# Linear attention: where the two transpositions of the next batch stand in TensorE's order, which engine copies them out, and three small products in one PSUM bank

## The chip, the cores and the metric

The kernel runs on one core of one Trainium2 chip. The metric is the device time of one execution in microseconds; the median of three runs of the kernel before is 1341.5 us (1340.82 to 1342.1).

## What is computed

A transformer-like block on `x` of shape (4, 512, 256), fp32 throughout: a mixture of experts, then linear attention added to `x`, then a softmax attention with a gate and a field term, then two layers of local attention with feed-forward, added to `x`. The change lies in the linear attention and in the first part ("front") of the attention that follows. Of the reference:

```python
qkv = x @ w_qkv.T                     # linear attention; x here: the experts' output
q, k, v = to_blocks(split(qkv))       # 8 heads of 32, blocks of 32 tokens
qp = elu(einsum('bhcsd,hdf->bhcsf', q, proj)) + 1.0
kp = elu(einsum('bhcsd,hdf->bhcsf', k, proj)) + 1.0
kv = einsum('bhcsf,bhcsd->bhcfd', kp, v)
num = einsum('bhcsf,bhcfd->bhcsd', qp, kv)
z = 1.0 / (einsum('bhcsf,bhcf->bhcs', qp, kp.sum(axis=3)) + 1e-08)
out = (num * z[..., None]) @ w_out.T + b_out
...
coh = sigmoid(tanh(comb @ Wc1.T + bc1) @ Wc2.T + bc2)   # next attention: the gate
mod = (1.0 - fi) * mod + fi * fa[:, None, :, None]      # the field term
```

## The kernel before

Stages follow one another: experts, linear attention, conditioned attention, local attention. The framework's list scheduler orders each engine's instructions at compile time from program order and its own estimate of when data are ready, and gives a tile the bank that it takes for free. TensorE is an exception: inside `PE.in_order()` every matmul and transposition keeps the program's order (L72 to L93). `pinned(...)` (L1215) holds one instruction behind the one that the program has just before it on its engine; it is a lower bound on its place, not an exact one.

The linear attention works on the 4 batches one after another. PSUM has 8 banks: 4 make up two double banks `fe` for features, 4 form the pool `mm` for all else (L1771, L1772).

`front(b)` (L1778) is a generator that prepares a batch in pieces, one for each `yield`: it combines the experts' results (`weighted`, `g` and `ymoe`), starts the loads for a later batch (`results`), then two turns (four transpositions each into a bank `pt`, copied to `yT`), four products `pqk` copied to `qk` (in the order 0, 2, 1, 3), and two products `pv` copied to `v`. `evac` (L124) gives these copies to ScalarE and VectorE in turn, so the first half of `yT` is copied by ScalarE and the second by VectorE.

The main loop (L1901) has a step `k` for each batch `b` and pair of heads `u` from 0 to 3. Its functions:

- `features(d, u)`: 4 products `pf` (32 rows each) into the two double banks; on ScalarE relu and exp for each (`ex`), on VectorE `f` from `pf` and `ex`. `f` frees the double bank.
- `scores(d, u)`: 8 products of 128 by 128 into two banks `psc`, masked on VectorE into `sc`.
- `values(d, g)`: the products `pn` and `pz` with `sc`, into one bank each; ScalarE copies `pz` to `z`, VectorE takes the reciprocal (3.35 us) and multiplies to `aT`. `pn` is held until then.
- `tail`: output product `pao` of a batch, added to `x`.

Between these the loop takes pieces from `fill`: the next batch's front and the last batch's tail (`beside`, L1879), or, in the last batch, the front of the conditioned attention for its batch 0 (`cond_front`, L285). An even step has three places (behind the values, behind the features, behind the scores), an odd one the last two: ten places for ten pieces. So a step with `u = 0` has, in TensorE's order: last values of the batch before, turn, features, turn, scores, first `pqk`. For the first batch these pieces stand elsewhere: its own `pv` take the first places and the next batch's turns come in step 1.

`cond_front` has two turns as well (copied to `xT2` by ScalarE for batch 0; VectorE sums the copies into `xs`), then products for keys, queries, gate and values. At its end stand small products: `pch` (the gate, L355), copied to `chT`; `pvs` (the sums of the values, L364), from which `vs` and `vsB` are made; `pchT` (the turn of `chT`, L373), from which `coh` is made; and `pvw` (L388) with `vsB`. Each takes a bank of its own through `acct`, which in this stage is the pool `mm`. Behind them TensorE has the last batch's last values, and then the next stage, whose scores `sc` have 5 banks and whose other products have 3.

## Time and profile before

| what | value |
| --- | --- |
| median of the runs | 1341.5 us (1340.82 to 1342.1) |
| the profiled execution: its own time | 1343.32 us |
| its span, first to last instruction | 1341.6 us |
| mean granted TensorE clock | 0.983 |
| linear attention in the span | about 305 to 465 us |
| reciprocal on 128x512 (L1856) | 3.35 us |
| copy of a turn: ScalarE, VectorE | 0.58, 0.68 us |
| relu and exp on 128x1024 (L1819, L1820) | 1.02, 1.06 us |
| `f` on 128x1024 (L1822) | 1.22 us |

A timeline row has the start in the span, the duration, the engine (PE is TensorE's matmul, PEld its weight load, DVE VectorE, ACT ScalarE, POOL GpSimd), the line, the operation, output and inputs by tile names, and the shape; in brackets stands the idle time before it and what ended it. Rows of like instructions are merged, with a count. A row of windows gives, for each stretch, its length, each engine's busy time and the granted clock. Products and transpositions go through helpers, so their lines are L82 and L86 and they are told apart by tiles.

### The profile page before, as it was taken

Reading aid. Unit: us, or ns where it says so; the run is one execution under the profiler, and the core shown is the slowest. Engines: PE = TensorE matmul, PEld = TensorE weight load, DVE = VectorE, ACT = ScalarE, POOL = GpSimd, SP = SyncE. Lnnn points to the kernel's source line nnn. Section 1 sums busy time; section 2 is a strip of 40 time slices with the busy share of each in tenths; the row PEclk is TensorE's granted clock in tenths of the full one; section 3 lists DMA queues with packets and bytes.
Section 4 is the critical chain, followed back from the end, with each engine's and each line's share of the span. In section 5 each row is a group of like instructions: output and inputs, shape, how many; then the busy total and the mean of one; then the engine's idle time right before and its main releaser. Section 6 shows DMA issues by size and latency. Waiting matters only on the chain.

```text
span 1341.6 us, 23073 instructions
## 1 busy us (share of the span) xinstructions
PE 1271.8 (95%) x9214; PEld 812.2 (61%) x9214; DVE 683.4 (51%) x1464; ACT 581.4 (43%) x1157; POOL 292.9 (22%) x321
## 2 busy tenths in 40 slices
PE   4899999998999999999999999999999998999998
PEld 3788899964566634344344655766555556667654
DVE  6221243425777733242237788654372877864421
ACT  3221233326655365646644646561222655463111
POOL 1322356420000101010103334210030333422010
PEclk7899999998999999999999999999999999999999
DMA  3565666523000000000210001311001011012000
GB/s 96 213 236 192 236 239 221 189 76 116 1 1 1 1 1 1 0 1 1 91 57 14 18 18 27 104 34 25 24 0 43 25 30 30 18 43 56 18 21 22
DMA packets 41856, 85.29 MB, mean 64 GB/s; under 512 B 9409, under 2 KB 25673, under 8 KB 39433
## 3 DMA queue, kind: packets, MB, share of 16 engines
q1 hardware_dynamic: 36600, 73.02, 16.9%
q0 software_dynamic: 3504, 9.46, 2.1%
q8 instruction: 77, 1.26, 0.4%
q10 hardware_dynamic: 1632, 1.21, 0.3%
q14 instruction: 43, 0.34, 0.1%
HBM read 74.76 MB, written 6.82 MB: 61 GB/s over the span
## 4 chain that ended last, share of the span: by engine, by line
PE 75%; DVE 9%; DMA 6%; ACT 5%; issue 3%; POOL 1%; SPq 0%; DVEq 0%; POOLq 0%
PE ph L82 11%; PE pdq L82 7%; PE pfy L82 6%; PE sc L82 6%; PE pua L82 5%; PE pug L82 5%; PE pv L82 5%; PE pdy L82 4%; PE po L82 3%; PE pn L82 3%; DMA ys<-ob,goal 2%; PE pds L82 2%; PE pqk L82 1%; PE pz L82 1%; PE pqt L86 1%
## 5 line engine op out<-in xcount | busy, mean ns | idle before, releaser
L82 PE MATMUL pdq<-wqkv,yT 128*128 128x512 f32 x384 | 171.7, 597 | 2.4 <-DVE t L626 2.2
L424 ACT ACTIVATE cex<-sc 128x512 f32<-128x512 f32 x256 | 132.2, 604 | 85.6 <-PE sc L82 84.6
L82 PEld LDWEIGHTS pdq<-wqkv,yT 128*128 128x128 f32 x384 | 71.1, 190 | 84.6 <-issue 76.1
L82 PE MATMUL ph<-h,w 128*128 128x256 f32 (+2 forms) x576 | 121.5, 370 | 0.3 <-ACT h L1596 0.3
L629 POOL TENSOR_TENSOR qr<-t,t 128x512 f32<-128x512 f32 x64 | 81.3, 1271 | 140.5 <-DVE t L626 140.5
L82 PEld LDWEIGHTS ph<-h,w 128*128 128x128 f32 x576 | 102.0, 192 | 15.2 <-ACT h L1596 0.5
L1461 DVE TENSOR_SCALAR h<-ph,w 128x256 f32<-128x256 f32 (+2 forms) x52 | 23.0, 461 | 121.8 <-PE ph L82 101.7
L394 POOL TENSOR_SCALAR fterm<-vw,faT 128x256 f32<-128x256 f32 x16 | 14.6, 920 | 317.6 <-DVE cr L384 317.6
L82 PE MATMUL sc<-qm,kT 32*128 32x512 f32 x512 | 82.6, 639 | 0.0
L681 ACT ACTIVATE p<-pds,ss 128x192 f32<-128x192 f32 (+1 forms) x256 | 79.8, 425 | 2.1 <-PE pds L82 0.8
L82 PE MATMUL pua<-hT,w 128*128 128x512 f32 x160 | 75.3, 593 | 0.9 <-DVE z L706 0.9
L82 PE MATMUL pug<-hT,w 128*128 128x512 f32 x160 | 76.2, 598 | 0.0
L619 ACT ACTIVATE sq<-pdq 128x512 f32<-128x512 f32 x64 | 38.5, 601 | 83.7 <-POOL qr L629 42.2
L714 POOL TENSOR_TENSOR p<-p 128x192 f32<-128x192 f32 x64 | 42.4, 682 | 138.1 <-PE pn L82 135.3
L796 ACT ACTIVATE gl<-pug,cols 128x512 f32<-128x512 f32 x40 | 27.3, 687 | 93.6 <-PE pug L82 90.8
L82 PE MATMUL pv<-cex,v 128*32 128x512 f32 x512 | 61.9, 598 | 2.7 <-DVE vw L391 2.7
L82 PE MATMUL pfy<-w,uA 128*128 128x256 f32 x256 | 61.4, 383 | 0.0
L82 PE MATMUL po<-w,h 128*128 128x256 f32 x264 | 60.1, 380 | 0.0
L82 PE MATMUL pdy<-wo,oT 128*128 128x256 f32 x256 | 58.9, 383 | 0.0
L684 DVE TENSOR_TENSOR p<-p,lmask 128x384 f32<-128x384 f32 x64 | 47.0, 735 | 23.0 <-ACT p L681 21.6
L82 PE MATMUL pn<-p,v 64*64 64x128 f32 (+1 forms) x1792 | 50.3, 254 | 8.2 <-DVE p L687 4.2
L1459 ACT ACTIVATE h<-ph,w 128x256 f32<-128x256 f32 (+2 forms) x52 | 22.4, 455 | 81.9 <-PE ph L82 78.0
(352 smaller groups left out, 2329.8 us busy)
## 6 DMA issues: line engine op xcount, KB each, us to landing
w<-in_moe_w_dram SPq DMA_DIRECT2D x18, 1024.0 KB, 7.9
w<-in_moe_w_dram SPq DMA_DIRECT2D x18, 516.0 KB, 4.0
w<-in_moe_w_dram SPq DMA_DIRECT2D x14, 640.0 KB, 4.5
zb<-rows SPq DMA_DIRECT2D x32, 256.0 KB, 4.1
g<-ys SPq DMA_DIRECT2D x6, 512.0 KB, 6.9
wqkv<-in_f_wqkv_dram SPq DMA_DIRECT2D x2, 1536.0 KB
w<-in_f_w_dram SPq DMA_DIRECT2D x2, 1408.0 KB
w<-in_moe_w_dram SPq DMA_DIRECT2D x4, 512.0 KB
```

Source lines behind the costliest of these rows:

```text
L82: cls._queue(nc.tensor.matmul(*args, **kw))
L86: cls._queue(nc.tensor.transpose(*args, **kw))
L394: nc.gpsimd.tensor_scalar_mul(fterm[:, t, :], vw, W["faT"][:, t, b : b + 1])
L424: nc.scalar.activation(ex[:, i, :], pss[2 * j + i], AF.Exp, scale=CHD**-0.5)
L619: nc.scalar.activation(sq, p3, AF.Square)
L629: nc.gpsimd.tensor_tensor(qr_t[:, s], t1, t2, ALU.add)
L681: nc.scalar.activation(p[:, j * 192 : j * 192 + n], pss[j // 2][r][:, j % 2 * 192 : j % 2 * 192 + n], AF.Exp, scale=d.ss[:, j, 1, 2 * c + ...
L684: nc.vector.tensor_tensor(edges, edges, lmask[:, :128].rearrange("p (s q) -> p s q", q=64).unsqueeze(1).to_broadcast([128, 3, 2, 64]), ALU ...
L714: nc.gpsimd.tensor_tensor(p[:, 1:, 0:64], p[:, 1:, 0:64], p[:, : NT - 1, 128:], ALU.add)
L796: nc.scalar.activation(gl, pg, AF.Gelu, bias=col("bg", l * (NU + 1) + i))
L1459: pinned(nc.scalar.activation(dst, src, AF.Relu, bias=bias))
L1461: pinned(nc.vector.tensor_scalar(dst, src, bias, 0.0, ALU.add, ALU.max))
```

## The change

Three edits. In `cond_front`, for batch 0, the sums and the turn of `chT` go to free columns of the bank that holds `pch`; other batches keep their banks. In `front`, the batches behind the first copy both turns by ScalarE, pinned. In the loop, the first step of each batch but the first takes two pieces directly behind the values and none behind the features, so that both turns stand ahead of the features.

```diff
-        ps = acct("pvs")
+        sums = ps[:, 128:130] if b == 0 else acct("pvs")[:, 0:2]
         for c in range(2):
-            mm(ps[:, c : c + 1],
+            mm(sums[:, c : c + 1],
                [(W["wqkv"][:, k, 2 * H + c * 128 : 2 * H + (c + 1) * 128], xs[:, k : k + 1]) for k in range(2)])
         vs = tile_of(temp, [128, 2], "vs")
-        nc.vector.scalar_tensor_tensor(vs, bv2, float(S), ps[:, 0:2], ALU.mult, ALU.add)
+        nc.vector.scalar_tensor_tensor(vs, bv2, float(S), sums, ALU.mult, ALU.add)
         vsB = tile_of(temp, [128, 2, 128], "vsB")
         nc.vector.tensor_copy(vsB, vs.unsqueeze(2).to_broadcast([128, 2, 128]))
         yield
-        ps = acct("pchT")
-        PE.transpose(ps[:, 0:128], chT, ident)
+        turned = ps[:, 256:384] if b == 0 else acct("pchT")[:, 0:128]
+        PE.transpose(turned, chT, ident)
         C3 = [128, NT, CH]
         coh = tile_of(keep, C3, "coh")
         nc.vector.tensor_tensor(
-            coh, ps[:, 0:128].rearrange("p (t h) -> p t h", h=32)[:, :, 0:CH],
+            coh, turned.rearrange("p (t h) -> p t h", h=32)[:, :, 0:CH],
             row("bc2").unsqueeze(1).to_broadcast(C3), ALU.add)
...
                         PE.transpose(pt[:, k * 128 : (k + 1) * 128], y[b][:, k, c * 128 : (c + 1) * 128], ident)
-                    evac(yT[:, c, :], pt)
+                    if b:
+                        pinned(nc.scalar.copy(yT[:, c, :], pt))
+                    else:
+                        evac(yT[:, c, :], pt)
                     yield
...
                         values(ds[b0], u0 // 2)
                         next(fill, None)
+                        if u == 0:
+                            next(fill, None)
                     if k + 1 < len(steps):
                         b1, u1 = steps[k + 1]
                         features(ds[b1], u1)
-                    next(fill, None)
+                    if u or k == 0:
+                        next(fill, None)
                     if b < B:
                         scores(ds[b], u)
                     next(fill, None)
```

## The prediction

> **What bounds the kernel now.** I read the page first, from the busy shares down:

> ```profile
> PE 1271.8 (95%) x9214; PEld 812.2 (61%) x9214; DVE 683.4 (51%) x1464; ACT 581.4 (43%) x1157; POOL 292.9 (22%) x321
> ```

> TensorE is the bound; VectorE and ScalarE matter only where TensorE waits for them. The linear-attention stage runs from about 305 to 465 us. So I next asked for the busy time in three of its stretches, each from one first turn to the next (the last ends at the last values):

> ```profile
> core 0: us, PE busy (x) PEld busy (x) DVE busy (x) ACT busy (x) POOL busy (x), PEclk, DMA share, GB/s
> 354.50:390.10 35.60, 33.41 (x285) 22.16 (x281) 25.83 (x26) 19.69 (x22) 0.00 (x0) 1.00 0.01 1
> 390.10:425.60 35.50, 33.34 (x281) 22.11 (x280) 25.83 (x26) 19.70 (x22) 0.00 (x0) 1.00 0.00 1
> 425.60:463.00 37.40, 35.63 (x247) 23.49 (x246) 27.82 (x34) 17.27 (x21) 0.00 (x0) 1.00 0.00 1
> ```

> The granted clock is full (1.00) and DMA is silent, so neither is in play. TensorE is idle 2.2, 2.2 and 1.8 us: 6.1 us in all. No reordering here can win more than about that, 0.45% of the kernel. Where it lies is in the timeline, TensorE first, from the first turn of the batch at 354.5 us:

> ```profile
> 354.50 0.66 PE L86 MATMUL pt<-ident,ymoe 128*128 128x128 f32 x4
> 355.08 1.14 PE L82 MATMUL pf<-qk,aproj 32*128 32x512 f32 x8
> 356.15 0.66 PE L86 MATMUL pt<-ident,ymoe 128*128 128x128 f32 x4
> 356.65 1.95 PE L82 MATMUL psc<-f 128*128 128x128 f32 x16
> 359.55 1.13 PE L82 MATMUL pqk<-yT,awqkv 128*128 128x512 f32 x2 [0.96 <-DVE aT L1857]
> 361.28 1.12 PE L82 MATMUL pqk<-yT,awqkv 128*128 128x512 f32 x2 [0.60 <-DVE yT L129]
> 362.34 1.29 PE L82 MATMUL pf<-qk,aproj 32*128 32x512 f32 x8
> ```

> The first product pqk waits twice: for a bank (pn's, free when aT is done) and for the second turn's copy. VectorE shows why both are late:

> ```profile
> 355.35 3.35 DVE L1856 RECIPROCAL z<-z 128x512 f32<-128x512 f32 x1 [1.94 <-ACT z L1851]
> 358.81 0.69 DVE L1857 TENSOR_TENSOR aT<-pn,z 128x512 f32<-128x512 f32 x1
> 359.42 1.22 DVE L1822 SCALAR_TENSOR_TENSOR f<-pf,ex 128x1024 f32<-128x1024 f32 x1
> 360.55 0.68 DVE L129 COPY yT<-pt 128x512 f32<-128x512 f32 x1
> 361.14 1.22 DVE L1822 SCALAR_TENSOR_TENSOR f<-pf,ex 128x1024 f32<-128x1024 f32 x1
> ```

> The copy, whose data are there at 356.8, stands behind the 3.35 us reciprocal. The boundary at 390.1 has the same waits (0.93 and 0.60).

> **The turns and their copies, boundaries at 354.5 and 390.1.** Nothing is added to TensorE: pt, pf, pt becomes pt, pt, pf, and psc still starts at 356.65. ScalarE gains a copy of 0.58 (its own first copy's row) in each of three batches, VectorE loses one of 0.68. No DMA is moved: the result loads are still issued with the first turn. The pin holds the first copy behind the batch's four g on ScalarE; all 16 of those are done by 321.6.

> ScalarE: second copy about 355.75 to 356.3; pf now ends 0.5 later, at 356.7, so the four passes of relu and exp start at 356.73 instead of 356.26 and end at 360.84 instead of 360.37. What is queued behind them are the two f on VectorE. The first f starts at 359.42 as before, because aT holds it. The second could start at 360.88; but between the two f the VectorE queue has a hole, where the compile-time list scheduler put the copy, and I expect it to put a masking (sc, 0.64) there. Then the second f stands at 361.16 to 362.38, as late as before.

> TensorE: psc takes 1.78 to the next start, so pqk starts at 358.43 (a turn's bank is free by 356.3) and is through at 360.34. That wins 2.0. But the next pf needs the two feature banks that the two f empty: its first half goes at 360.69, its second at 362.43. A split pf is seen in the row of the third boundary below: its second half starts at 433.85 and the next piece 1.06 later. So the next pqk starts at 363.49 instead of 363.56: the wait for a bank and a copy turns into a wait for f, and the win shrinks to 0.07 here.

> It comes back one step on. The first half's features are ready at 361.83, so relu starts at 361.87 instead of 363.51; four passes later (365.98 instead of 367.63) the last f ends at about 367.3 and the maskings at 368.5 instead of 370.08. The values before waited for these: 368.98 to 372.00, 3.02 us, against 1.88 without a wait (352.61 to 354.49). Now they start at 368.91, wait for nothing and end at 370.79: **1.2 us won at each of the two boundaries, -2.4 together**. Bounds for each: 0.6 if both maskings go ahead of the second f (362.98), 1.5 if none does. If pqk still gets pn's bank and waits to 359.5, the same counting gives 0.9. The following odd step has its own stall of about 1.2 (values at 388), set by the chain from its own pf; it moves along and gives nothing.

> **The third boundary, 425.6.** Here the fill is the first front of the next attention; its copies are ScalarE's already.

> ```profile
> 431.00 1.98 PE L82 MATMUL pck<-xT,cwqkv 128*128 128x512 f32 x4 [1.27 <-DVE aT L1857]
> 432.91 2.07 PE L82 MATMUL pf<-qk,aproj 32*128 32x512 f32 x8
> ```

> pck can start at 429.56 and loses its wait, but VectorE works from 426.46 to 435.0 without a hole: reciprocal, xs 0.63, aT, f, xs 0.68, f (432.59 to 433.80), maskings. All of it but the maskings stands ahead of the second f in the new order too, so pf's second half still starts at 433.85. Value 0; bounds -0.6 (an xs behind the f) and +0.6 (a masking ahead of it).

> **The first batch's copy (330 to 336).** The slots don't move; the second copy leaves VectorE (334.94 to 335.62) for ScalarE, idle from 333.8 to 335.96. The product that reads it starts at 335.79 after the values. Value 0, bounds 0.3 either way.

> **Three products in one bank.**

> ```profile
> 460.24 1.05 PE L82 MATMUL pvs<-xs,cwqkv 128*128 128x1 f32 x8
> 460.38 0.28 DVE L361 COPY chT<-pch 128x128 f32<-128x128 f32 x1
> 461.16 0.31 PE L86 MATMUL pchT<-ident,chT 128*128 128x128 f32 x1
> 461.33 0.16 DVE L369 SCALAR_TENSOR_TENSOR vs<-cols,pvs 128x2 f32<-128x2 f32 x1 [0.66 <-PE pvs L82]
> ```

> Before, pvs is written while chT is read, in two banks. By these rows the sharing costs nothing. [...] Behind pvw on TensorE stand the last values. [...] I take **+0.5**. A gain could come only from a bank that is free earlier: pvw's wait of 0.50 ends with coh, and vsB is done at 461.81, so at most 0.1.

> **The handover to the next stage.** With two fewer banks taken, the last pn and pz may lie in other banks. The next stage's second score waits 0.58 for z now, its second turn 0.59 for aT. Value 0; bounds -1.2 (both waits gone) and +3.9 (the slower rival below).

> **Sum:** -2.4 + 0 + 0 + 0.5 + 0 = -1.9 us. The profiled execution has a span of 1341.6 and a time of its own of 1343.3; the median is 1341.5. A difference of 1.9 is the same against either, so from the median: **1339.6 us**.

> **Rivals.** A difference of 0.2% (2.7 us) is about what a measurement of this kernel can tell from no change.
> - *More is freed* (chance 0.25): no masking ahead of the second f (1.5 twice), and one handover wait gone (0.6) or an xs behind its f. -3.0 + 0.5 - 0.6 = -3.1: 1338.4; with everything, -4.3: 1337.2. For it: VectorE is idle enough. Against: the queue fills that hole in the rows shown.
> - *The change doesn't do what it says* (0.17): f takes the whole of the place of the removed waits, because both maskings go ahead. -1.2 + 0.5: 1340.8. For it: in the first batch (332.60) two maskings do stand ahead of the second f. Against: there a copy stood between relu and exp and made the hole wider.
> - *Slower* (0.13): the next stage's second score, released at 465.71 by z, gets pn's bank instead. That one is free only when aT is done at 469.71, behind 3.4 us of reciprocals. TensorE keeps its order, so it stands 4.0 longer: -1.9 + 4.0 = +2.1, 1343.6. It decides from a wait over 1.9. For it: the second turn waits for that bank now, so the scheduler hands it out too early. Against: only one of the four banks goes to the scores.
> - The forecast itself has 0.45, with its own bounds 1338.4 to 1340.8.

> Range 1337.0 to 1342.4: from everything freed to the nearer part of the slower case. Faster by over 0.2% (below 1338.8): most of the first rival and a fourth of my own case, 0.33. Slower (above 1344.2): only the slower rival with a further cost, 0.09. Within: 0.58.

> **What the changed profile would show.** Right: pqk without a wait at the first two boundaries, the next pf split in two by a wait for f of about 1.7 us, and the values one step on taking 1.9 us instead of 3.0; pvs starting after chT's end. Wrong: pqk still waiting for aT or yT; a stretch from first turn to first turn shorter by much more than 1.2 us, or not at all; a gain in the third stretch; a new wait of sc or pt for aT after 463 us. All would be wrong if the schedule of later stages changed.

## The result, and the profile after

The changed kernel takes 1343.3 us (median of 21 runs, 1341.38 to 1346.93); the kernel before, run in turn with it, takes 1341.2 us (21 runs, 1335.94 to 1342.16). The ratio is 1.0023, with a 95% interval of 1.0016 to 1.003: slower by about 0.2%, and the interval leaves out no change. The forecast was 1339.6, a little faster.

The profiled execution of the changed kernel has a span of 1342.7 us and a time of its own of 1344.44. The three stretches that the prediction shows look, in the windows view, much as before, but for one figure (columns: start and end, length, busy time of TensorE, its weight load, VectorE, ScalarE and GpSimd with counts, granted clock, DMA share, GB/s):

```profile
354.50:390.10 35.60, 33.69 (x311) 22.64 (x304) 25.21 (x25) 20.18 (x23) 0.00 (x0) 1.00 0.00 1
390.10:425.60 35.50, 33.62 (x246) 21.45 (x243) 25.07 (x25) 20.18 (x23) 0.00 (x0) 0.95 0.00 1
425.60:463.00 37.40, 35.75 (x294) 23.95 (x282) 26.74 (x30) 17.02 (x20) 0.00 (x0) 1.00 0.01 2
```

In the second row the clock is 0.95, where before all three rows had 1.00. More of TensorE's time is busy than before in both of the first two rows (33.69 against 33.41, 33.62 against 33.34); in the second, part of that is work at half speed. I come back to this.

First the order of the work. TensorE's timeline at the first boundary of the changed kernel (this profile runs 0.80 us later here than that of before; lines from `front` on have moved by 3):

```profile
355.30 1.09 PE L86 MATMUL pt<-ident,ymoe 128*128 128x128 f32 x8
356.33 1.14 PE L82 MATMUL pf<-qk,aproj 32*128 32x512 f32 x8
357.40 2.05 PE L82 MATMUL psc<-f 128*128 128x128 f32 x16
359.29 1.88 PE L82 MATMUL pqk<-yT,awqkv 128*128 128x512 f32 x4
361.49 1.13 PE L82 MATMUL pf<-qk,aproj 32*128 32x512 f32 x4 [0.32 <-DVE f L1825]
363.91 1.13 PE L82 MATMUL pf<-qk,aproj 32*128 32x512 f32 x4 [1.29 <-DVE f L1825]
```

Both turns stand together, `pqk` waits for nothing, and the next `pf` is split in two by a wait for `f` (1.29 us, where about 1.7 was expected): signs that the prediction named. So is the next one, the values one step on, from `pn` to the product behind them in 1.89 us instead of 3.02:

```profile
370.38 0.42 PE L82 MATMUL pn<-sc,v 128*32 128x128 f32 x8
372.27 1.98 PE L82 MATMUL pqk<-yT,awqkv 128*128 128x512 f32 x4
```

VectorE shows how late the second `f` is:

```profile
359.62 0.69 DVE L1860 TENSOR_TENSOR aT<-pn,z 128x512 f32<-128x512 f32 x1
360.22 1.21 DVE L1825 SCALAR_TENSOR_TENSOR f<-pf,ex 128x1024 f32<-128x1024 f32 x1
361.36 1.28 DVE L1835 TENSOR_TENSOR sc<-psc,bmask 128x512 f32<-128x512 f32 x2
362.55 1.21 DVE L1825 SCALAR_TENSOR_TENSOR f<-pf,ex 128x1024 f32<-128x1024 f32 x1
```

Between the two `f` stand both maskings (x2, 1.28), not one. The second `f` begins at 362.55, with the 0.80 taken off 0.6 us later than I had it.

The small products at the end of the stage, TensorE, changed kernel:

```profile
460.91 0.64 PE L82 MATMUL pch<-cT,cwc 128*32 128x128 f32 x16
461.96 1.05 PE L82 MATMUL pch<-xs,cwqkv 128*128 128x1 f32 x8 [0.41 <-DVE chT L361]
463.27 0.33 PE L86 MATMUL pch<-ident,chT 128*128 128x128 f32 x1 [0.25 <-DVE vs L369]
463.60 1.13 PE L82 MATMUL pvw<-cwout,vsB 128*128 128x256 f32 x4
```

All three go to one tile, and each waits until VectorE has read the one before: the sums begin 0.06 us after `chT`'s end (461.90). Before, `pvw` waited 0.50 for `coh` in the same place, so the net price is 0.40. Behind them the next stage's second score and second turn, which waited 0.58 and 0.59 before, wait for nothing now. Of the kernel before, `pvw` and the second turn:

```profile
461.96 1.10 PE L82 MATMUL pvw<-cwout,vsB 128*128 128x256 f32 x4 [0.50 <-DVE coh L377]
469.76 0.66 PE L86 MATMUL pt<-ident,xres 128*128 128x128 f32 x4 [0.59 <-DVE aT L1857]
```

and of the changed kernel, the second turn:

```profile
472.00 0.66 PE L86 MATMUL pt<-ident,xres 128*128 128x128 f32 x4
```

To sum this up I compared the start of the same instruction in both timelines at each end of a part, and took off 1.7 us for each stretch of half speed within it (below). By the order of its work the changed kernel wins 1.1 at the first two boundaries and 0.2 at the third, loses 0.4 at the small products and wins 0.8 at the handover: -1.7 us. Yet it is slower. Ahead of these parts and behind them, half speed taken off in the same way, the profiles don't tell the two kernels apart: up to the first turn at 354.5 the kernel before takes 339.1 us and the changed kernel 338.2 and 340.2 in two profiles (the second is e5's), and from the handover to the end 863.1 against 863.4 and 861.5. Executions of one kernel differ by 2 us there, so a smaller change of order elsewhere is not excluded. What the records do show is the clock.

### The profile page after: what moved, and what is told of

Read it like the earlier page. It is cut to its first block, busy times and chain, and to the rows that moved or that the text cites. A ratio compares the mean times of both kernels' runs of the same rounds, so it can differ in the third digit from the quotient of the medians.

```text
span 1342.7 us, 23072 instructions
## 1 busy us (share of the span) xinstructions
PE 1275.4 (95%) x9214; PEld 814.3 (61%) x9214; DVE 682.0 (51%) x1461; ACT 582.7 (43%) x1160; POOL 292.9 (22%) x321
## 3 DMA queue, kind: packets, MB, share of 16 engines
q0 software_dynamic: 3504, 9.46, 2.1%
## 4 chain that ended last, share of the span: by engine, by line
PE 77%; DVE 9%; DMA 6%; ACT 4%; issue 2%; POOL 0%; SPq 0%; DVEq 0%; POOLq 0%
PE ph L82 11%; PE pdq L82 7%; PE pfy L82 6%; PE sc L82 6%; PE pua L82 5%; PE pug L82 5%; PE pv L82 5%; PE pdy L82 4%; PE po L82 3%; PE pn L82 3%; DMA ys<-ob,goal 2%; PE pqk L82 2%; PE pds L82 2%; PE pqt L86 1%; PE pz L82 1%
## 5 line engine op out<-in xcount | busy, mean ns | idle before, releaser
L82 PE MATMUL pdq<-wqkv,yT 128*128 128x512 f32 x384 | 171.7, 596 | 2.4 <-DVE t L626 2.2
L82 PEld LDWEIGHTS pdq<-wqkv,yT 128*128 128x128 f32 x384 | 71.0, 190 | 84.6 <-issue 76.1
L82 PE MATMUL ph<-h,w 128*128 128x256 f32 (+2 forms) x576 | 121.3, 369 | 0.3 <-ACT h L1596 0.3
L82 PEld LDWEIGHTS ph<-h,w 128*128 128x128 f32 x576 | 101.7, 192 | 15.4 <-ACT h L1596 0.5
L82 PE MATMUL sc<-qm,kT 32*128 32x512 f32 x512 | 82.7, 641 | 0.0
L82 PE MATMUL pua<-hT,w 128*128 128x512 f32 x160 | 75.3, 593 | 1.2 <-DVE z L706 1.2
L82 PE MATMUL pug<-hT,w 128*128 128x512 f32 x160 | 76.1, 598 | 0.0
L82 PE MATMUL pv<-cex,v 128*32 128x512 f32 x512 | 61.9, 598 | 2.7 <-DVE vw L391 2.7
L82 PE MATMUL pfy<-w,uA 128*128 128x256 f32 x256 | 61.4, 383 | 0.0
L82 PE MATMUL po<-w,h 128*128 128x256 f32 x264 | 60.1, 380 | 0.0
L82 PE MATMUL pdy<-wo,oT 128*128 128x256 f32 x256 | 59.3, 384 | 0.0
L82 PE MATMUL pn<-p,v 64*64 64x128 f32 (+1 forms) x1792 | 50.3, 254 | 7.2 <-DVE p L684 3.5
```

Of the source, the lines that this page charges most:

```text
L82: cls._queue(nc.tensor.matmul(*args, **kw))
```

## Where the time went: the clock

TensorE's granted clock falls to half in two places of the changed kernel's stage: from 400.2 and from 465.0 us. In the profile of before it does so nowhere between 335 and 480 us. The windows view, asked for stretches of 3.41 us, of the changed kernel:

```profile
396.77:400.18 3.41, 2.12 (x9) 0.56 (x8) 2.36 (x4) 2.53 (x4) 0.00 (x0) 1.00 0.00 0
400.18:403.59 3.41, 3.41 (x5) 1.33 (x5) 0.87 (x1) 1.99 (x2) 0.00 (x0) 0.50 0.00 0
461.62:465.03 3.41, 2.82 (x29) 2.16 (x33) 1.78 (x8) 0.26 (x1) 0.00 (x0) 1.00 0.00 0
465.03:468.44 3.41, 3.41 (x64) 3.02 (x56) 1.08 (x4) 0.40 (x1) 3.10 (x4) 0.50 0.00 0
```

and of the kernel before, at its emptiest place of the first boundary:

```profile
358.00:361.41 3.41, 1.85 (x9) 0.83 (x8) 3.31 (x5) 2.34 (x3) 0.00 (x0) 1.00 0.00 0
361.41:364.82 3.41, 3.41 (x13) 1.32 (x14) 2.14 (x3) 1.86 (x3) 0.00 (x0) 1.00 0.00 0
```

In the second row of the first fence five rows of products fill 3.41 us. The `pqk` there takes 3.62 us, against 1.98 one boundary earlier:

```profile
364.97 1.98 PE L82 MATMUL pqk<-yT,awqkv 128*128 128x512 f32 x4
399.98 3.62 PE L82 MATMUL pqk<-yT,awqkv 128*128 128x512 f32 x4
```

The busy share doesn't tell what releases it. The window at 358.0 of before was busy for 1.85 us and nothing followed; the one at 396.8 of after was busy for 2.12, its longest gap 1.29, and half speed followed. What differs is what the products do. A row of `psc` streams 128 columns, and 16 rows take 1.78 us to the next start: 0.87 ns per column; four rows of `pqk` with 512 columns take 1.82: 0.89. With 0.88, four rows of `pqk` count 4 x 512 x 0.88 ns = 1.80 us; but the four rows of half a `pf` have 32 rows where `pqk` has 128 (`32*128` and `128*128` in the timeline), so I count them as 1.80 / 4 = 0.45 us, in 1.13 of busy time. Added up over a window and divided by 3.41 this gives an activity, which is my estimate from the shapes and these times (products with 32 columns where `pqk` has 128 are weighted likewise, and a row across an edge is shared by its time on each side). The window at 396.8 is two halves of `pf` with waits around them: 0.26. The one at 358.0 has `psc` and `pqk` in it: 0.44. These are the windows of the grid between 335 and 1331 us in 13 traces (before, after and eleven experiments), without those that are themselves at half speed:

| activity of a window | followed by half speed |
| --- | --- |
| under 0.30 | 31 of 31 |
| 0.30 to 0.35 | 8 of 10 |
| 0.35 to 0.40 | 6 of 17 |
| 0.40 to 0.45 | 1 of 22 |
| 0.45 to 0.60 | 0 of 164 |
| over 0.60 | 0 of 3504 |

The counts in the middle rows move by a few with the way in which a row across an edge is shared. Laid on every place of the grid, the table gives an estimate of how many half-speed stretches an execution of the changed kernel has between 335 and 480 us: 2.0 and 1.8 from its two profiles (1.2 to 1.4 at the first two boundaries, 0.4 at the third, 0.3 at the small products), which is 3.1 to 3.5 us, against 0.04 for the kernel before. The table comes from the same traces, so this checks the size alone.

The waits on the split `pf` are short, at most 1.29 us; still the changed kernel loses up to 1.7 us, by the estimate above, each time that a window of an activity under 0.30 falls there (0.26 at 396.8).

Since the grid lies elsewhere in each execution, one profile can't give the cost. The mean over runs can: each run has its granted clock, and I take span times (1 - clock) as the clock time that it lost. Within one kernel, a lost us goes with 0.68 us of time (254 runs of 11 kernels, correlation 0.69), so taking all of it is an upper measure. In the runs of e5 (below), which have the clock for both, the kernel before lost 18.7 us (35 runs) and the changed kernel 22.1 (12 runs): 3.4 more. With -1.7 from the order that makes +1.7, or +0.6 with 0.68 of it; measured were +2.4 in the mean (+0.7 to +4.4).

## The experiments

The columns of this table: the order's sum (as above, from one profile, clock taken off), the difference in lost clock time (mean over runs), their sum, and the measured difference of the means from the kernel before, all in us; then the ratio with its interval, which is not the ratio of the means. Each has 6 to 22 runs, against 29 to 36 of before on the same chip (e1 to e4 on one, e5 to e8 on a second, e9 to e11 on a third).

| kernel | order | clock | sum | measured | ratio |
| --- | --- | --- | --- | --- | --- |
| e5: the changed kernel again | -1.7 | +3.4 | +1.7 | +2.4 | 1.0019 (1.0005 to 1.0033) |
| e1: turns alone | -0.5 | +4.5 | +4.1 | +5.1 | 1.0039 (1.0025 to 1.0052) |
| e2: shared bank alone | -0.4 | +1.3 | +0.9 | +1.2 | 1.0003 (0.9994 to 1.0012) |
| e3: e1, maskings last | +0.6 | +3.3 | +3.9 | +3.7 | 1.0031 (1.0021 to 1.0041) |
| e4: idle products, banks moved | +2.0 | +4.7 | +6.7 | +8.5 | 1.0065 (1.0052 to 1.0078) |
| e6: idle products, banks kept | -1.7 | +1.0 | -0.7 | +1.1 | 1.0005 (0.9991 to 1.0019) |
| e7: maskings last, two boundaries | -3.6 | +1.6 | -2.0 | -2.1 | 0.9983 (0.9969 to 0.9997) |
| e8: changed, maskings last | -2.8 | +3.2 | +0.4 | +0.1 | 0.9997 (0.9985 to 1.001) |
| e9: copies alone | -0.7 | +0.5 | -0.2 | +0.7 | 1.0011 (0.9995 to 1.0027) |
| e10: places alone | -1.7 | +1.9 | +0.2 | 0.0 | 1.0001 (0.9984 to 1.0018) |
| e11: e7 again | -3.6 | +1.2 | -2.4 | -2.2 | 0.9991 (0.9977 to 1.0005) |

Order and clock together come within 1.0 us of the measured difference in nine of the eleven rows; e4 and e6, the two with idle products, miss it by 1.8.

All but e2 are given as edits of the changed kernel, unless another is named.

**e1: the turns alone.** The three small products keep their banks.

```diff
-        sums = ps[:, 128:130] if b == 0 else acct("pvs")[:, 0:2]
+        sums = acct("pvs")[:, 0:2]
...
-        turned = ps[:, 256:384] if b == 0 else acct("pchT")[:, 0:128]
+        turned = acct("pchT")[:, 0:128]
```

> The early turns with ScalarE's copies, each small product in its own bank as before. My theory: the changed kernel loses by TensorE's clock. Both maskings stand ahead of the second f, so pf is split by a wait of 1.3 us between two halves that use only half of the array's rows, and in some executions the next clock window of 3.4 us is granted half speed, which costs 1.7 us; 0.5 us is won at each of the first two boundaries. Then this kernel stands between -1 and +1.5 us of the kernel before, with a half-speed window between 360 and 405 us in some profiles, and below the changed kernel by 0.5 to 2. Rival: the sharing of the bank, and what it does to the banks of the next stage, is the whole loss. Then this kernel is 1.1 us faster than before.

A miss: it is the slowest but one, 5.1 us over before, and slower than the changed kernel, not faster. The boundaries give what they gave (-1.1, and -0.4 at the third), but at the handover the next stage's first turn now waits for `aT`, since it was given the bank of `pn`:

```profile
467.87 1.12 PE L86 MATMUL pt<-ident,xres 128*128 128x128 f32 x4 [2.87 <-DVE aT L1860]
```

and the profile has four windows at half speed between 335 and 480 us, two of them from 466.4 us on, as it ends. (The halves of `pf` work on 32 rows where `pqk` works on 128: a quarter, not half.)

**e2: the shared bank alone**, as an edit of the kernel before: only the lines of `cond_front`.

```diff
-        ps = acct("pvs")
+        sums = ps[:, 128:130] if b == 0 else acct("pvs")[:, 0:2]
...
-        ps = acct("pchT")
+        turned = ps[:, 256:384] if b == 0 else acct("pchT")[:, 0:128]
```

> Only the shared bank; turns and copies as before. My theory: the wait for chT and for vs costs 0.4 us on TensorE, and the window of the small products (at about 460 us) becomes a half-speed candidate, so +0.4 to +2 us against the kernel before. Rival (the sharing is the whole loss): +3 us in every execution, with a wait behind the handover to the next stage. Third possibility (sharing frees banks and the handover waits go): within 0.3 us.

The order loses 0.4 at the small products and wins 0.8 at the handover, as in the changed kernel: both belong to this edit. Its profile has one half-speed stretch there, from 464.9 us, behind the small products, as in the changed kernel, and it loses 1.3 us more to the clock. By the ratio's interval the time can't be told from before.

**e3: the maskings behind the second `f`**, on e1, in the first step of the batches behind the first.

```diff
-                    nc.vector.tensor_tensor(sc, psc.rearrange("p (t q) -> p t q", q=128), cw_["bmask"], ALU.mult)
+                    masked = nc.vector.tensor_tensor(sc, psc.rearrange("p (t q) -> p t q", q=128), cw_["bmask"], ALU.mult)
+                    if u == 0 and d is not ds[0]:
+                        pinned(masked)
```

> The early turns without the shared bank, and the two maskings of the first step of each later batch pinned behind the second f. My theory: the second f ends 1.2 us earlier, the split of pf shrinks to less than 0.5 us of wait in its second half, each of the first two boundaries wins 1.3 to 1.5 us, no half-speed window there: 2 to 3 us faster than the kernel before. If the order of f and the maskings were not the failing step, it stands like the early turns alone, within 0.5 us.

A miss: a faster kernel was expected, and it is 3.7 us over before. The boundaries did gain: -3.0 for the first two instead of -1.1. But the next stage's second score was given `pn`'s bank. TensorE's timeline of e3 at the handover:

```profile
457.58 1.12 PE L82 MATMUL sc<-qm,kT 32*128 32x512 f32 x2
462.56 1.41 PE L82 MATMUL sc<-qm,kT 32*128 32x512 f32 x6 [3.85 <-DVE aT L1862]
```

This is the slower rival of the prediction (4.0 there, 3.85 here), in another kernel than the one that it was written for.

**e4: idle products in the hole**, a first trial of the clock: three times five products of `ident` with itself, each five in a bank of their own, between the two halves of the split `pf` at the first two boundaries and ahead of `pf` at the third.

```diff
+            def warm(n):
+                t = mmt("pwarm")
+                for _ in range(n):
+                    PE.matmul(t[:, 0:128], ident, ident, start=True, stop=True)
...
+                    if u == 2 and d is not ds[0] and s == (d is not ds[3]):
+                        warm(5)
```

> The changed kernel with 15 more matmuls of 128 by 128 on the identity matrix, whose result nobody reads: 5 in the wait between the halves of pf in each of the first two boundaries and 5 ahead of pf in the third, about 1.1 us each, so that TensorE works while it would wait. If half-speed windows are what it loses: 1 to 3 us faster than the changed kernel, although it does more work, and no half-speed window at 360 to 440 us. If the clock has no part: as slow as the changed kernel or up to 0.5 us slower.

Also a miss in the time, which says little of the clock: the three extra tiles turned the banks, the second score waits 3.9 us for `aT` as in e3, and the kernel is 8.5 us over before, of which 1.8 stay unaccounted for. As expected, though, its profile has no half speed between 335 and 460 us; two windows of it lie at the wait, from 465.2.

**e5: the changed kernel again**, unedited, to stand beside e6 to e8.

> The changed kernel once more, as a base for the three kernels of this job. Reading of the traces so far: the order of the program is about 1.2 us shorter than before, and half-speed clock windows cost 3.6 us more than before. Then it is 2 to 3 us slower than before again, its mean granted clock is lower by 0.002 to 0.003, and the half-speed windows of its profile lie at other places of the three boundaries and of the handover than in the first profile.

+2.4 in the mean, 1342.2 in the median. In this profile half speed falls on the first boundary instead of the second, behind a window at 362.9 that was busy for 2.11 of 3.40 us: the same place in the work, another place of the grid.

**e6: idle products, banks kept.** Five at each of the first two boundaries, and one into a bank of its own ahead of the sums, which turns the banks back to where the changed kernel has them.

```diff
+        if b == 0:
+            PE.matmul(acct("spare")[:, 0:128], ident, ident, start=True, stop=True)
... (`warm` as in e4)
+                    if u == 2 and s == 1 and (d is ds[1] or d is ds[2]):
+                        warm(5)
```

> The changed kernel with five idle matmuls between the halves of pf at the first two boundaries, and one more into a bank of its own ahead of pvs, which turns the banks so that the last pn and pz lie in the same two as in the changed kernel (in the first kernel with idle matmuls pn lay in the bank of the next stage's second score). If the clock is what the changed kernel loses at these boundaries: 1.5 to 3 us faster than the changed kernel in this job, though TensorE does 11 matmuls more, and the mean clock higher by 0.001 to 0.002. If not: equal or slower by up to 0.5 us.

TensorE's timeline of e6 at the first boundary, where the hole is filled (five products give ten rows) and the second half of `pf` begins no later:

```profile
360.16 1.13 PE L82 MATMUL pf<-qk,aproj 32*128 32x512 f32 x4 [0.33 <-DVE f L1834]
361.22 1.38 PE L82 MATMUL pwarm<-ident 128*128 128x128 f32 x10
362.57 1.13 PE L82 MATMUL pf<-qk,aproj 32*128 32x512 f32 x4
```

The order is that of the changed kernel, and TensorE has 11 products more to do. The clock time lost falls from 22.1 to 19.7 us (by 2.5, interval 0.8 to 4.1, from resampling the runs), and the median from 1342.2 to 1340.7. In its profile no half speed follows the first two boundaries; two such stretches lie at the third, where nothing was added. So work in the hole of the split `pf` gives clock back; one of the 11 products stands among the small products and may have a small part in it. That the time falls with it is likely, not shown: the difference of the means is -1.3, interval -3.0 to +0.4, and 1.8 us of e6 stay unaccounted for.

**e7: maskings behind `f`, first two boundaries only, no shared bank.** Built from e3 by giving the last batch its old places back.

```diff
-                        if u == 0:
+                        if u == 0 and b < B - 1:
                             next(fill, None)
...
-                    if u or k == 0:
+                    if u or k == 0 or b == B - 1:
                         next(fill, None)
```

> Maskings pinned behind the second f, the early turns at the first two boundaries only, each small product in its own bank. The last pn and pz now lie in banks that the next stage asks for late, where the same order with all three boundaries had pn in the bank of the second score and stood 3.8 us there. If banks and clock explain that kernel's loss: 1.4 us won at each of two boundaries, both handover waits gone (0.8), no half-speed window added: 3 to 4 us faster than before, 1337 to 1338.5. If the pin itself were the loss: slower than before again.

The profile of e7, TensorE at the first boundary (it starts 0.12 later than in the changed kernel's):

```profile
359.40 1.88 PE L82 MATMUL pqk<-yT,awqkv 128*128 128x512 f32 x4
361.61 1.13 PE L82 MATMUL pf<-qk,aproj 32*128 32x512 f32 x4 [0.33 <-DVE f L1825]
363.04 1.13 PE L82 MATMUL pf<-qk,aproj 32*128 32x512 f32 x4 [0.31 <-DVE f L1825]
```

and VectorE there:

```profile
360.34 1.21 DVE L1825 SCALAR_TENSOR_TENSOR f<-pf,ex 128x1024 f32<-128x1024 f32 x1
361.76 1.22 DVE L1825 SCALAR_TENSOR_TENSOR f<-pf,ex 128x1024 f32<-128x1024 f32 x1 [0.21 <-ACT ex L1823]
362.91 1.28 DVE L1835 TENSOR_TENSOR sc<-psc,bmask 128x512 f32<-128x512 f32 x2
```

The wait in the split `pf` is 0.31 instead of 1.29, each boundary gives 1.5, no window of the stage is followed by half speed, and the banks fall such that neither the score nor the turn waits at the handover. 1337.4 us against 1340.0 of before: faster, by 2.1 in the mean, where 3 to 4 was expected. It still loses 1.6 us more clock than before (e11 1.2), though the estimate from the table above gives it only 0.2: some 1 us of its lost clock comes from places that I have not found.

**e8: the changed kernel with the maskings behind `f`**, and nothing else (e3's edit).

> The changed kernel with the maskings pinned behind the second f and nothing else: the one step undone that the prediction got wrong. Won: 1.4 us at each of the first two boundaries; paid: 0.4 for the shared bank, 0.2 at the third boundary; the second turn of the next stage waits for pn's bank as before (0.6), the second score no longer for z. By order 2.5 us faster than before; about 0.6 half-speed windows more on average (third boundary, shared bank), 1 us. So 1 to 2.5 us faster than before and 3.5 to 5 faster than the changed kernel.

1339.9 us: 2.3 us under e5 in the mean (0.9 to 3.7), but 0.1 over before, where it was expected under it. The boundaries win 3.0, but the handover wins nothing here, since the next stage's second turn waits for `aT`:

```profile
467.59 0.63 PE L86 MATMUL pt<-ident,xres 128*128 128x128 f32 x4 [1.08 <-DVE aT L1862]
```

Lost clock is no less than in e5 (21.9 and 22.1), so what e8 wins on e5 is the order's. That does not fit smoothly: e8 has no long wait in the split `pf` at the first two boundaries, and the estimate from the table gives it 2.1 us over before, while 3.2 were measured. As in e7, about 1 us stays open.

**e9 and e10: the two halves of the early turns.** e9 keeps the copies by ScalarE and gives the turns their old places; e10 keeps the places and gives the second copy back to VectorE. Neither shares the bank. The edit of e10, on top of e1's:

```diff
-                    if b:
-                        pinned(nc.scalar.copy(yT[:, c, :], pt))
-                    else:
-                        evac(yT[:, c, :], pt)
+                    evac(yT[:, c, :], pt)
```

> Only the copies: both on ScalarE, pinned; the second turn stands behind the features as before, no shared bank, and pn and pz end in the same banks as before. The second copy now stands behind the four passes of relu and exp and ends at about 361.0 instead of 361.2; pqk still waits for aT's bank. Nothing is won or lost at the boundaries (0 to 0.3 us each), no half-speed window is added: within 0.7 us of the kernel before. If moving the copy off VectorE were what wins, 1 us faster or more.

> Only the places: both turns ahead of the features, the second still copied by VectorE, no shared bank, pn and pz in the same banks as before. The second copy stands behind the reciprocal (359.4), pqk waits about 1 us for it in one piece, f is later by 0.6 and the next pf splits. By order 0 to 0.5 us faster than before over the stage; the split pf makes half-speed windows possible at all three boundaries (about 1 more on average): 0 to +2.5 us.

e9 wins 0.36 at each boundary: `pqk` still waits 0.96 for a bank, but its second part waits 0.22 for ScalarE's copy instead of 0.60 for VectorE's. e10 wins 0.78 at each, more than the two edits together (0.55), since in its profile one masking (0.68) stands between the two `f` and the other behind them. Yet e10's time is that of before: it loses 1.9 us more to the clock. Neither alone makes the kernel slower; neither makes it faster.

**e11: e7 again**, on another chip.

> The kernel with the maskings behind the second f and early turns at two boundaries, once more, since its interval reached to within 0.03% of no change: 2 to 4 us faster than before again.

1337.9 us, 2.4 below before in the median; by itself its interval includes no change. The 24 runs of e7 and e11 together are 2.1 us under the 64 of before (1.2 to 3.1). This is the version that beats both kernels: the early turns where they help, the maskings out of the way of `f`, and nothing shared.

## Why the prediction was wrong, point by point

- **What bounds the kernel: the step that failed.** "The granted clock is full (1.00) and DMA is silent, so neither is in play." That held for the order before, and I carried it over to an order that I was about to change. The prediction even described what half speed followed here: a `pf` split in two by a wait (1.29 us measured, about 1.7 forecast), work on 32 rows instead of 128 with holes around it (activity 0.26). The missing term is +3.4 us of clock, against a sum of -1.9 for everything else. By the estimate above most of it belongs to the split `pf`; a part belongs to the small products in one bank, whose half-speed stretch is in both profiles of the changed kernel and in e2's. Shown: half speed follows these windows, the clock over many runs is lower (e5), and filling the hole gives 2.5 us of it back (e6). Not settled: how much of the lost clock becomes time (0.68 to all of it), which leaves 0.7 to 1.8 of the +2.4 us open; and about 1 us of lost clock in e7 and e8 that the split `pf` does not explain.
- **First two boundaries, -2.4.** Right in kind, half in size: -1.1. The path was as written (no wait for a bank or a copy; the split `pf`; the values one step on in 1.89 us instead of 3.02). The mis-sized term is "I expect it to put a masking (sc, 0.64) there": it put both there, 1.28. That was the bound of 0.6 for each, which I had also put under a rival. e3, e7 and e8 put them behind `f` and measured 1.5 for each: the upper bound, too, was right.
- **Third boundary, 0.** -0.2, within the bounds; the wait went to the next `pf`, 1.23 us, but in one piece ahead of it, since the second `xs` now stands ahead of both `f`.
- **The first batch's copy, 0.** Right: the changed profile runs 0.81 us later at the `pf` ahead of these values (328.94 against 328.13) and still 0.81 at the product behind them (336.60 against 335.79).
- **Three products in one bank, +0.5.** +0.4, in both the changed kernel and e2. The +0.5 was a guess of mine: no row of before shows a wait for a shared bank, and by those rows it was 0. The runs show that the compiled program waits, although the columns are disjoint: the sums begin 0.06 us after `chT`'s end. Whether it does so for the bank or because all three lie in one tile, no run separates. What the term left out is the clock: e2 loses 1.3 us of it.
- **The handover, 0 (bounds -1.2 and +3.9).** -0.8: both waits went. What sets it is which bank `pn` and `pz` lie in at the end of the stage. By the banks in the built programs, the next stage's second score takes bank 4, its first turn 5 and its second 7; `pn` lies in 7 before, in 6 after, in 5 in e1 (turn waits 2.87), in 4 in e3 and e4 (score waits 3.85 and 3.9), in 7 again in e8 (second turn waits 1.08). Edits far from there move it.
- **The rivals.** "The change doesn't do what it says" had the VectorE queue right, both maskings ahead. "Slower" told of a wait that came in e3 (3.85) and e4 (3.9), and not in the changed kernel. No rival had the clock, so none of the cases held the cause, and the range ended below the result.

Together: the order gave about what I had summed, with other terms, and the clock took more than that back, up to twice as much.

## What to carry to other kernels

A reordering that removed idle time (-1.7 us by its order) lost here (+2.4 in the mean of e5) where it gathered thin work (few rows, few columns, holes) into one short stretch: work out the activity, as above, of any 3.41 us of a new order (here half speed followed all 31 windows under 0.30 and none over 0.45), and compare the mean granted clock of many runs, not one profile (here 0.981 and 0.983 in one profile of the changed kernel each, 0.983 in that of before; in the mean of the runs 0.9835 against 0.9860). When a stall moves to another wait, see which operations stand ahead of what now decides, and put them behind it; here that won 1.9 us at the first two boundaries, on top of 1.1 for the reordering itself. Edits that took or freed a bank moved the banks of the next stage here (its score or turn waited from 0 to 3.9 us), so read its first waits before crediting the edit.

## What the runs showed that I had not expected

- Half speed came in stretches of 3.41 us, or two of them, behind windows in which TensorE was busy for 62% (2.12 of 3.41) and 83% (2.82) of the time. The second one holds small products: sums with one column each, a single turn, `pvw`, and the first values, 32 columns wide; its activity is 0.38. By the activity above no window over 0.45 was followed by it, every one under 0.30 was (31).
- Between these figures the outcome is mixed (15 of 49), so the activity as I worked it out does not decide alone.
- The banks that the scheduler hands out at the end of a stage are worth from -0.8 to +3.8 us at the next one, for kernels that differ by one edit elsewhere.
